# Graph-network layer: the overflow of two grouped quads in one accumulation, and remainders, ranks, splits and lists at other places of the hand-written order

## The chip, the cores and the metric

The kernel runs on one core of a Trainium2 chip. A core has five engines that run side by side, each with a queue of its own in program order: TensorE (PE, with PEld for its weight loads), VectorE (DVE), ScalarE (ACT), GpSimd (POOL) and SyncE (SP, which here only issues DMAs). The metric is device microseconds of one launch, as the median of several runs. The profile is of one further execution of the same program.

## What is computed

The reference is one message-passing layer on a graph of 6,250 nodes and 200,000 edges, sorted by `dst`:

```python
h = relu(layernorm(x)) @ W_in
W_ij = (softplus_shifted(f_ij @ W_f1 + b_f1) @ W_f2 + b_f2) * f_ij_cutoff
out = segment_sum(h[dst] * W_ij, src, 6250)      # a random scatter-add of 200,000 rows of 128
result = x + softplus_shifted(out @ W_o1 + b_o1) @ W_o2 + b_o2
```

`edge_index` is `[src, dst]`, so the messages are gathered by the sorted index and summed by the random one. The scatter-add of 200,000 rows of 128 numbers is what most of the kernel is about.

## The kernel before

**Items.** The edges are cut into 391 quads of 512 edges (four chunks of 128). The main loop (from line 1220 on) runs over items `i`. In item `i` the quads near `i` are each at another stage: `s1_*` makes the softplus of the edge features of quad `i` (PE `z` on line 326, ACT on lines 331 and 336), `s2_*` the message of quad `i-1` (PE `xg` and `W` on lines 507 to 518, ACT `xc` on line 523, and on line 533 the product of `W` and `xc` on DVE, `s2_m`), `s3_*` the rest of quad `i-2` to `i-4`. What else has to run is hung on an item and on a point of it with `at(item, point, function)`: L (loads), D0, D1, A0, A1, DM, PE2, A2, D2, S, run in this order of the code. The order is kept as written on every engine, so a function that is hung on an early point stands ahead of everything that comes later in the item on its engine.

**Three ways to sum a message.** 31 quads are plain: equal sources inside a chunk are summed with a matmul and each chunk is added into DRAM with one indirect DMA of POOL (line 595). 192 quads are listed: each of their four chunks is added with one such DMA straight from the product, and duplicate sources are moved into a list of 128 rows that is summed on its own (`l_*`; `l_eq` on line 382 compares, two instructions for four quads). 168 quads are grouped, with no DMA of their own: 128-row chunks are sorted on TensorE into 16 groups of 32 slots by a one-hot matrix `pm` (`perm_oh`, `permute`, line 700), and every eight of them make a round of four units (`unit_oh`, `unit_pe` on line 794, `unit_evac` on line 805) that add 32 slots of each group into the SBUF table `accT`. All indirect adds go through one POOL queue: 987 DMAs in the run.

**The grid of nine.** Grouped quads start at item 8 with gaps of 2, 2, 2 and 3. With phase = (item - 8) mod 9 they are at the phases 0, 2, 4 and 6. Units sit in items of phase 2 and 6 (`UOFF`); `clear` pushes a step to the next item that has no unit.

**The functions around the change.** A grouped quad `q` gets its product in item `q+1` into `pt` (two buffers, `part_new`). The product is kept as three bf16 pieces that lie in the high halves of f32 numbers: `part_rem` (line 689) makes two remainders, in item `q+2` at D2, and `part_ext` adds three index columns; a row of `pt` then has 387 columns. `permute` runs in the items `q+3` and `q+4`. Slots beyond the 16 x 32 go to 64 overflow slots of the quad: `over_pe` (lines 708 to 718) sums the three pieces of each of four chunks with twelve matmuls of 64 columns of weights into one half of a PSUM tile, `over_out` copies 64 x 131 numbers to one half of `mo`, and after every second grouped quad `over_idx`, `over_dg`, `over_row`, `over_eq`, `over_sum` (line 754, f32) and `over_scatter` sum equal rows of `mo` and add them to DRAM with one DMA. PSUM tiles of the tag `B` have four buffers, which `permute`, the units, the overflow and most side work share.

**The side work.** `rank_group`, `rank_count`, `rank_own`, `rank_over`, `rank_slot` make the slots of eight grouped quads at once, ahead of the first of them. `fb_load`, `fb_1` to `fb_4` split 4,096 edges' features in three bf16 pieces every eight items; `fb_2` also takes their largest absolute value (line 287). `unit_oh` makes the eight one-hot matrices of a unit, four two items ahead and four one item ahead. A list's `l_eq` and `l_count` run in the first items that have its data.

Of the kernel before, what the change touches and what calls it, by code (L numbers as in the profile page):

```python
# [54 lines left out]
def tile_gnn(ctx: ExitStack, tc: tile.TileContext, x, fB, cT, srcT, srcr, dstr, win_, wf1, wf2, bias, bo1c, wo1,  # L55
# [113 lines left out]

    def zero_list(k, j):  # L170
        v = accs[k][ACC_R:].rearrange("(p t) f -> p (t f)", p=P)
        w = LR // ZL
        nc.sync.dma_start(v[:, j * w:(j + 1) * w], zero[:, :w])

    def rows(t, o, T):
        n = min(T, 2)
# [104 lines left out]
    def fb_1(b):  # L281
        f3 = wk.tile([P, 3, FE], BF16, tag="f3", name="f3", bufs=2)
        nc.scalar.copy(f3[:, 0], fst[b]["f"])
        fst[b]["f3"] = f3

    def fb_2(b):
        nc.vector.tensor_reduce(fmax[:, b:b + 1], fst[b]["f"], axis=AX.X, op=ALU.max, apply_absolute_value=True)
# [418 lines left out]
        nc.scalar.copy(mp[q]["ms", s][:, :PW], mp[q].pop(("q", s))[:, :PW])  # L706

    def over_pe(q):
        h = mpi[q] % 2 * OVC
        t = ps.tile([P, 512], F32, tag="B", name="po", bufs=4)  # L710
        o = t[h:h + OVC]
        for c in range(4):
            w = mp[q]["pm"][:, c, GRP * CAP:]
            pt = high(mp[q]["pt"][:, c:c + 1])[:, 0]
            nc.tensor.matmul(o[:, :P + 3], w, pt[:, 2 * P:PW], start=(c == 0), stop=False)  # L715
            nc.tensor.matmul(o[:, :P], w, pt[:, P:2 * P], start=False, stop=False)  # L716
            nc.tensor.matmul(o[:, :P], w, pt[:, :P], start=False, stop=(c == 3))  # L717
        mp[q]["po"] = t

    def over_out(q):  # L720
        h = mpi[q] % 2 * OVC
        mo = mos[mpi[q] // 2 % 2]
        nc.scalar.copy(mo[h:h + OVC, :P + 3], mp[q].pop("po")[h:h + OVC, :P + 3])

    def over_none(q):
        nc.vector.memset(mos[mpi[q] // 2 % 2][OVC:, :P + 3], 0.0)

    def over_idx(q):
        mo = mos[mpi[q] // 2 % 2]
        so = sp_.tile([P, 1], F32, tag="ovs", name="ovs", bufs=3)  # L730
        nc.vector.scalar_tensor_tensor(so, mo[:, P + 2:P + 3], float(GN), mo[:, P + 1:P + 2], op0=ALU.mult, op1=ALU.add)
        mp[q]["so"] = so

    def over_dg(q):
# [10 lines left out]
        mp[q]["row"] = t  # L745

    def over_eq(q):
        eq = wk.tile([P, P], F32, tag="oeq", name="oeq", bufs=1)
        nc.vector.tensor_scalar(eq, mp[q].pop("row")[:, :P], mp[q]["so"], None, op0=ALU.is_equal)
        mp[q]["eq"] = eq  # L750

    def over_sum(q):
        t = ps.tile([P, 512], F32, tag="B", name="osum", bufs=4)
        nc.tensor.matmul(t[:, :P + 4], mp[q]["eq"], mos[mpi[q] // 2 % 2][:, :P + 4], start=True, stop=True)
        mp[q]["sum"] = t

    def over_copy(q):
# [91 lines left out]
    with tc.manual_schedule():  # L849
# [70 lines left out]
        fb_1(0)  # L920
        prep_norm(0)
        prep_tp(0)
        fb_2(0)
        prep_relu(0)
        prep_mm(0)
# [22 lines left out]
            nc.vector.tensor_copy(m_[:, :, 128:129], wgt.unsqueeze(1).to_broadcast([P, 4, 1]))  # L948
            ms.append(m_)
        for mo_ in mos:  # L950
            nc.vector.tensor_copy(mo_[:, P + 3:P + 4], wgt)
        idl = cp.tile([P, max(NW, 1)], F32, name="idl")
        iotl = cp.tile([P, P + LCAP], F16, name="iotl")
        nc.vector.tensor_scalar(iotl, iotw[:, GN // 2:GN // 2 + P + LCAP], float(LCAP - 1), None, op0=ALU.subtract)
# [183 lines left out]
        for w in range((LE - LB) // SW):  # L1138
            for g in range(4):
                n = LB + SW * (w - 1) + 4 * g  # L1140
                i = splain[n] + 2 if w else 6 + 2 * g
                for k in range(2):
                    kk = (LB + SW * w + 4 * g) // 2 + k
                    at(max(0, i + k - 2), "L", sb_load, kk)
                    at(i + k, "DM", l_eq, kk)
                i = clear(i + 2, units)
                at(i, "PE2", l_count, (LB + SW * w) // 4 + g)
                at(i + 1, "D0", l_dup, w, g)
            i += 1
# [12 lines left out]
            at(i, "PE2", over_row, ("L", w))  # L1162
            at(i + 1, "D0", l_same, w)
            k = clear(i + 1, units)
            at(k - 1, "L", l_load, w)
            at(k, "PE2", l_sum, w)
            at(k + 1, "A0", l_copy, w)
            at(k + 1, "DM", l_ji, w)
            at(k + 1, "A2", over_int, ("L", w))
            at(k + 2, "S", over_scatter, ("L", w))  # L1170
# [3 lines left out]
                    at((0, 3, 6, 9)[k] + j + 1, "L", zero_list, k, j)  # L1174
        for q in mpq:
            at(q + 1, "D2", perm_oh, q)
            at(q + 2, "D2", part_rem, q, 1)
            at(q + 2, "D2", part_rem, q, 2)
            at(q + 2, "A2", part_ext, q)
            if q + 4 in units:  # L1180
                for s in range(4):
                    at(q + 3, "PE2", permute, q, s)
                for s in range(4):
                    at(q + 3, "PE2", perm_out, q, s)
                at(q + 3, "PE2", over_pe, q)
                at(q + 3, "PE2", over_out, q)
# [6 lines left out]
            if q == mpq[-1] and mpi[q] % 2 == 0:  # L1193
                at(q + 4, "D2", over_none, q)
# [25 lines left out]
        for i in range(max(NQ + 7, last + 16, r0_end + 2, lend + 24)):  # L1220
# [396 lines left out]
```

## Time and profile before

| | |
|---|---|
| median of 3 runs | 2064.37 us (2062.51 to 2069.87) |
| the profiled execution's own time | 2051.26 us |
| its span | 2049.5 us |
| PE, DVE, ACT, POOL busy | 1855.4, 1658.4, 1491.2, 1636.9 us |
| mean granted TensorE clock | 0.966 |
| indirect adds of POOL (line 595) | 987, of 1.59 to 1.64 us each |
| permutation matmuls (line 700) | 2688, 533.6 us |
| overflow matmuls (lines 715 to 717) | 3 x 672, 131.3 + 127.2 + 127.4 us |

Busy times of PE are modelled ends of pipelined matmuls and overlap; the distance from one start to the next tells what a matmul takes of the engine. "Issue" after an idle time means that the engine waited for nothing that the profile shows. A row of the timeline has the start in us, the length in us, the engine, the line, the operation, its tiles and shapes, how many were merged, and in brackets the idle time ahead of it and what ended it.

### The profile page before, as it was taken

How to read it: one execution, taken by the hardware profiler on the slowest of the kernel's cores; microseconds unless marked ns; L12 is line 12 of the kernel's file. 1: busy time of each engine (PE TensorE's matmuls, PEld its weight loads, DVE VectorE, ACT ScalarE, POOL GpSimd, SP SyncE). 2: the span in 40 equal slices, each digit the busy share in tenths (PEclk: the TensorE clock that was granted, in tenths of full speed). 3: DMA queues.
4: the chain of work that ended last, by engine and by line, in shares of the span. 5: the costliest groups of instructions: out<-in, count | busy, mean ns of one | idle time of the engine just before them, and what ended most of it. 6: DMA issues, size and time to landing. Idle time of an engine off the chain costs nothing. (4 is left out here: it accounts for less than half of the span.)

```text
span 2049.5 us, 57496 instructions
## 1 busy us (share of the span) xinstructions
PE 1855.4 (91%) x20381; PEld 1284.7 (63%) x20381; DVE 1658.4 (81%) x4449; ACT 1491.2 (73%) x4083; POOL 1636.9 (80%) x1040
## 2 busy tenths in 40 slices
PE   3579999999999999999999999999999999999966
PEld 2456666666666666666666666666666666677734
DVE  4578898798888888988888978879898887787745
ACT  3468776877777788777778777777877778788714
POOL 3578888888888888887878778888888888888884
PEclk9689999999999999999999999999999999999987
DMA  6887666667666676766667666676676666666747
GB/s 239 228 210 154 124 123 121 129 110 140 126 126 119 118 139 119 131 127 120 120 121 132 120 117 123 110 125 127 121 131 108 129 126 109 112 123 125 141 44 252
DMA packets 359686, 272.58 MB, mean 133 GB/s; under 512 B 97727, under 2 KB 319850, under 8 KB 359394
## 3 DMA queue, kind: packets, MB, share of 16 engines
q0 software_dynamic: 143728, 71.30, 34.9%
q1 hardware_dynamic: 215378, 197.50, 32.9%
q8 instruction: 161, 2.64, 0.5%
q14 instruction: 131, 1.07, 0.2%
q10 hardware_dynamic: 288, 0.07, 0.0%
HBM read 154.45 MB, written 114.24 MB: 131 GB/s over the span
## 5 line engine op out<-in xcount | busy, mean ns | idle before, releaser
L595 POOL DMA_INDIRECT acc<-s,lji x768 | 1242.7, 1618 | 254.5 <-issue 185.8
L700 PE MATMUL pq<-pt,pm 128*128 128x387 bf16 x2688 | 533.6, 342 | 33.6 <-DVE pt L689 10.5
L523 ACT ACTIVATE xc<-xg,cb 128x128 f32<-128x128 f32 x1564 | 447.7, 372 | 111.5 <-PE xg L510 101.8
L518 PE MATMUL W<-w,a 128*128 128x128 f32 x3128 | 465.3, 293 | 0.0
L518 PEld LDWEIGHTS W<-w,a 128*128 128x128 f32 x3128 | 389.6, 196 | 42.3 <-issue 3.1
L706 ACT CAST mst<-pq 128x387 bf16<-128x387 f32 x672 | 303.7, 482 | 135.0 <-PE pq L700 132.3
L700 PEld LDWEIGHTS <-pm 128*128 128x128 bf16 x2688 | 261.0, 99 | 221.5 <-issue 26.6
L794 PE MATMUL un<-so,mst 32*128 32x392 bf16 x8064 | 371.0, 326 | 12.9 <-DVE pr L640 6.4
L794 PEld LDWEIGHTS <-mst 32*128 32x128 bf16 x8064 | 223.9, 93 | 153.4 <-issue 51.0
L336 ACT ACTIVATE a<-a,con 128x512 f32<-128x512 f32 x391 | 282.3, 722 | 12.8
L331 ACT ACTIVATE a<-z 128x512 f32<-128x512 f32 x391 | 237.8, 608 | 32.9 <-PE z L326 18.0
L595 POOL DMA_INDIRECT acc<-s,ji x123 | 196.0, 1594 | 78.7 <-issue 26.5
L689 DVE TENSOR_TENSOR pt<-pt 128x512 f32<-128x512 f32 x336 | 231.7, 689 | 5.8
L675 DVE TENSOR_SCALAR pm<-iot,pos 128x576 bf16<-128x576 f16 x672 | 221.0, 390 | 0.0
L533 DVE TENSOR_TENSOR s<-W,xc 128x512 f32<-128x512 f32 x192 | 131.9, 687 | 89.1 <-ACT xc L523 84.9
L805 DVE TENSOR_TENSOR accT<-un,accT 128x392 f32<-128x392 f32 x320 | 158.5, 558 | 55.1 <-PE un L794 55.0
L779 DVE TENSOR_SCALAR so<-iot,mst 128x392 bf16<-128x392 f16 x672 | 192.6, 346 | 5.4 <-PE un L794 5.3
L595 POOL DMA_INDIRECT acc<-os,oji x96 | 156.9, 1635 | 30.7 <-issue 15.6
L510 PE MATMUL xg<-wn,oh 63*128 63x128 bf16 x1564 | 157.5, 222 | 14.8 <-ACT xc L523 8.2
L326 PE MATMUL z<-ft,ws 123*128 123x512 bf16 x391 | 151.9, 389 | 15.7 <-POOL b2rep L940 9.3
L507 PE MATMUL W<-b2rep,onesb 64*128 64x512 bf16 x391 | 154.1, 394 | 0.0
L533 DVE TENSOR_TENSOR pt<-W,xc 128x512 f32<-128x512 f32 x168 | 115.3, 686 | 44.1 <-ACT xc L523 36.0
(210 smaller groups left out, 2431.3 us busy)
## 6 DMA issues: line engine op xcount, KB each, us to landing
rb<-reld SPq DMA_DIRECT2D x391, 64.0 KB
fsd<-f SPq DMA_DIRECT2D x49, 480.0 KB
ft<-fsd SPq DMA_DIRECT2D x195, 120.0 KB
sb<-src SPq DMA_DIRECT2D x169, 128.0 KB
fb<-in_fB_dram SPq DMA_DIRECT2D x49, 320.0 KB
ft<-fsd SPq DMA_DIRECT2D x195, 80.0 KB
wn<-tab SPq DMA_DIRECT2D x782, 15.8 KB
acc<-s,lji POOLq DMA_INDIRECT x768
```

What stands on the lines that cost most here:

```text
L331: nc.scalar.activation(a, st[q]["z"], AF.Exp)
L336: nc.scalar.activation(a, a, AF.Ln, bias=half, scale=0.5)
L518: nc.tensor.matmul(W[:, c, :], st[q]["a"][:, c * P:(c + 1) * P], w2, start=False, stop=(c == 3))
L523: nc.scalar.mul(xc[:, c, :], st[q]["xg"][:, c, :], late["c", q // CQ][:, 4 * (q % CQ) + c:4 * (q % CQ) + c + 1])
L533: nc.vector.tensor_tensor(m[:, :, :P], st[q]["W"], st[q]["xc"], op=ALU.mult)
L595: nc.gpsimd.indirect_dma_start(out=accs[k][:rows, :], out_offset=bass.IndirectOffsetOnAxis(ap=ji, axis=0), in_=s, in_offset=None, compute_ ...
L675: nc.vector.tensor_scalar(pm[:, c], iot[:, :SLOTS], rk[r]["pos"][:, 4 * j + c:4 * j + c + 1], None, op0=ALU.is_equal)
L689: nc.vector.tensor_tensor(pt[:, :, k * P:(k + 1) * P], a, high(a), op=ALU.subtract)
L700: nc.tensor.matmul(t[:, :PW], mp[q]["pm"][:, c, s * P:(s + 1) * P], high(mp[q]["pt"][:, c:c + 1, :PW])[:, 0], start=(c == 0), stop=(c == 3))
L706: nc.scalar.copy(mp[q]["ms", s][:, :PW], mp[q].pop(("q", s))[:, :PW])
L779: nc.vector.tensor_scalar(so, iotw[:, :GN], w[:, 3 * P // 2:3 * P // 2 + 1], None, op0=ALU.is_equal)
L794: nc.tensor.matmul(ts[g][:, :GN], mp[q]["ms", s][v, k * P:(k + 1) * P], mp[q]["oh"][v], start=(q == qs[0] and k == 0), stop=(q == qs[-1] a ...
```

## The change

- `over_pe` runs once for two grouped quads (84 times): for each of the four chunks one matmul of 387 columns per quad, the first quad into the lower and the second into the upper 64 partitions of the PSUM tile, so that the matmuls go to the two halves of the array's columns in turn. The three pieces are no longer added in PSUM.
- `over_out` copies all 387 columns of both quads at once to `mo`, which becomes bf16; `over_sum` adds the three pieces with three bf16 matmuls; the one-hot `oeq` becomes bf16. `over_none` goes.
- `over_pe` and `over_out` move to a new point PE1, behind `s2_m` and ahead of `s3_pe`, of the item after the next grouped quad (phases 5 and 1). `part_rem` moves from D2 to a new point DR, right behind the product.
- `rank_group`, `rank_count` and `rank_own` run one item sooner.
- The maximum of the splits becomes `fb_max` and runs three items ahead of `fb_2`; the loads come six items ahead and no longer three; the splits start one item ahead of a unit, the lists' compares in a unit's item.
- The first half of `unit_oh` moves to the item of the second half for units of phase 6.
- The launch asks for `dynamic_dma_scratch_size=8192`, where before it named no size.

```diff
-        mo_ = cp.tile([P, 132], F32, name=f"mo{i}")
+        mo_ = cp.tile([P, PW + 1], BF16, name=f"mo{i}")
...
     def over_pe(q):
-        h = mpi[q] % 2 * OVC
+        qs = mpq[mpi[q] // 2 * 2:mpi[q] + 1]
         t = ps.tile([P, 512], F32, tag="B", name="po", bufs=4)
-        o = t[h:h + OVC]
         for c in range(4):
-            w = mp[q]["pm"][:, c, GRP * CAP:]
-            pt = high(mp[q]["pt"][:, c:c + 1])[:, 0]
-            nc.tensor.matmul(o[:, :P + 3], w, pt[:, 2 * P:PW], start=(c == 0), stop=False)
-            nc.tensor.matmul(o[:, :P], w, pt[:, P:2 * P], start=False, stop=False)
-            nc.tensor.matmul(o[:, :P], w, pt[:, :P], start=False, stop=(c == 3))
-        mp[q]["po"] = t
+            for h, p in enumerate(qs):
+                nc.tensor.matmul(t[h * OVC:(h + 1) * OVC, :PW], mp[p]["pm"][:, c, GRP * CAP:],
+                                 high(mp[p]["pt"][:, c:c + 1, :PW])[:, 0], start=(c == 0), stop=(c == 3))
+        mp[q]["po"] = t, len(qs) * OVC
...
     def over_out(q):
-        nc.scalar.copy(mo[h:h + OVC, :P + 3], mp[q].pop("po")[h:h + OVC, :P + 3])
+        nc.scalar.copy(mo[:n, :PW], t[:n, :PW])
...
     def over_sum(q):
-        nc.tensor.matmul(t[:, :P + 4], mp[q]["eq"], mos[mpi[q] // 2 % 2][:, :P + 4], start=True, stop=True)
+        nc.tensor.matmul(t[:, :P + 4], mp[q]["eq"], mo[:, 2 * P:], start=True, stop=False)
+        nc.tensor.matmul(t[:, :P], mp[q]["eq"], mo[:, P:2 * P], start=False, stop=False)
+        nc.tensor.matmul(t[:, :P], mp[q]["eq"], mo[:, :P], start=False, stop=True)
...
         for b in range(1, NB):
-            t0 = 2 if b == 1 else 8 * b - 8
+            t0 = 2
             if b > 1:
-                at(max(0, t0 - 3), "L", fb_load, b)
+                t0 = 8 * b - 8
+                while (t0 - MP0 + 1) % sum(MPGAPS) not in UOFF:
+                    t0 -= 1
+                at(max(0, t0 - 6), "L", fb_load, b)
+            at(max(t0 - 3, 1), "D2", fb_max, b)
...
-            at(i - 5, "D2", rank_group, r)
-            k = clear(i - 4, units)
-            at(k, "PE2", rank_count, r)
-            at(k + 1, "D0", rank_own, r)
-            k = clear(k + 1, units)
+            i = max(i, 6)
+            at(i - 6, "D2", rank_group, r)
+            at(i - 5, "PE2", rank_count, r)
+            at(i - 4, "D0", rank_own, r)
+            k = mpq[RKQ * r] if i == 6 else i - 2
             at(k, "PE2", rank_over, r)
             at(k + 1, "D0", rank_slot, r)
...
                 i = splain[n] + 2 if w else 6 + 2 * g
+                while w and (i - MP0) % sum(MPGAPS) not in UOFF:
+                    i -= 1
...
-            at(q + 2, "D2", part_rem, q, 1)
-            at(q + 2, "D2", part_rem, q, 2)
+            at(q + 2, "DR", part_rem, q, 1)
+            at(q + 2, "DR", part_rem, q, 2)
...
-                at(q + 4, "PE2", over_pe, q)
-                at(q + 5, "A0", over_out, q)
...
             if mpi[q] % 2 or q == mpq[-1]:
+                k = mpq[mpi[q] + 1] + 1 if mpi[q] + 1 < len(mpq) else q + 3
+                at(k, "PE1", over_pe, q)
+                at(k, "PE1", over_out, q)
...
-                at(k - 2, "D2", unit_oh, r, s, 0)
+                at(k - (1 if (k - MP0) % sum(MPGAPS) == UOFF[1] and k < last else 2), "D2", unit_oh, r, s, 0)
...
                 s3_idx(i - 3)
+            run(i, "DR")
+            run(i, "PE1")
...
-    nc = bacc.Bacc("TRN2", target_bir_lowering=False, num_devices=1)
+    nc = bacc.Bacc("TRN2", target_bir_lowering=False, num_devices=1, dynamic_dma_scratch_size=8192)
```

More of the change, by code (lines that the diff above doesn't have):

```diff
@@ L171, in zero_list @@
         v = accs[k][ACC_R:].rearrange("(p t) f -> p (t f)", p=P)
-        w = LR // ZL
-        nc.sync.dma_start(v[:, j * w:(j + 1) * w], zero[:, :w])
+        a, b = j * LR // ZL, (j + 1) * LR // ZL
+        nc.sync.dma_start(v[:, a:b], zero[:, :b - a])
     def rows(t, o, T):
@@ L284, in fb_1, with fb_max @@
         fst[b]["f3"] = f3
+    def fb_max(b):
+        nc.vector.tensor_reduce(fmax[:, b:b + 1], fst[b]["f"], axis=AX.X, op=ALU.max, apply_absolute_value=True)
     def fb_2(b):
-        nc.vector.tensor_reduce(fmax[:, b:b + 1], fst[b]["f"], axis=AX.X, op=ALU.max, apply_absolute_value=True)
         fr = wk.tile([P, FE], F32, tag="fr", name="fr", bufs=1)
@@ L708, in over_pe @@
     def over_pe(q):
[L709 removed]
+        qs = mpq[mpi[q] // 2 * 2:mpi[q] + 1]
         t = ps.tile([P, 512], F32, tag="B", name="po", bufs=4)
[L711 removed]
         for c in range(4):
[L713 to L718 removed]
+            for h, p in enumerate(qs):
+                nc.tensor.matmul(t[h * OVC:(h + 1) * OVC, :PW], mp[p]["pm"][:, c, GRP * CAP:],
+                                 high(mp[p]["pt"][:, c:c + 1, :PW])[:, 0], start=(c == 0), stop=(c == 3))
+        mp[q]["po"] = t, len(qs) * OVC
     def over_out(q):
[L721 removed]
+        t, n = mp[q].pop("po")
         mo = mos[mpi[q] // 2 % 2]
[L723 to L726 removed]
+        nc.scalar.copy(mo[:n, :PW], t[:n, :PW])
+        if n < P:
+            nc.vector.memset(mo[n:, :PW], 0.0)
     def over_idx(q):
@@ L730, in over_idx @@
         so = sp_.tile([P, 1], F32, tag="ovs", name="ovs", bufs=3)
-        nc.vector.scalar_tensor_tensor(so, mo[:, P + 2:P + 3], float(GN), mo[:, P + 1:P + 2], op0=ALU.mult, op1=ALU.add)
+        nc.vector.scalar_tensor_tensor(so, mo[:, PW - 1:PW], float(GN), mo[:, PW - 2:PW - 1], op0=ALU.mult, op1=ALU.add)
         mp[q]["so"] = so
@@ L747, in over_eq @@
     def over_eq(q):
-        eq = wk.tile([P, P], F32, tag="oeq", name="oeq", bufs=1)
+        eq = wk.tile([P, P], BF16, tag="oeq", name="oeq", bufs=1)
         nc.vector.tensor_scalar(eq, mp[q].pop("row")[:, :P], mp[q]["so"], None, op0=ALU.is_equal)
@@ L922, in tile_gnn @@
         prep_tp(0)
+        fb_max(0)
         fb_2(0)
@@ L950, in tile_gnn @@
         for mo_ in mos:
-            nc.vector.tensor_copy(mo_[:, P + 3:P + 4], wgt)
+            nc.vector.tensor_copy(mo_[:, PW:PW + 1], wgt)
         idl = cp.tile([P, max(NW, 1)], F32, name="idl")
@@ L1184, in tile_gnn @@
                     at(q + 3, "PE2", perm_out, q, s)
-                at(q + 3, "PE2", over_pe, q)
-                at(q + 3, "PE2", over_out, q)
             else:
```

3 lines of the change are left out of this document (1 added, 2 removed).

## The prediction, made before the result was known

> **What bounds the kernel now.** The page comes first, for the sizes, then the stretches of the run by engine, then what POOL waited for in each.
>
> ```profile
> span 2049.5 us, 57496 instructions
> PE 1855.4 (91%) x20381; PEld 1284.7 (63%) x20381; DVE 1658.4 (81%) x4449; ACT 1491.2 (73%) x4083; POOL 1636.9 (80%) x1040
> ```
>
> PE looks like the bound and POOL, at 80%, does not. But the page does not count a gap that POOL has between every two indirect adds. The stretches (length; then busy us and instructions of PE, PEld, DVE, ACT, POOL; granted clock, DMA share, GB/s) and POOL's waits (us, times, longest) in the first of them:
>
> ```profile
> 150.00:1206.00 1056.00, 991.19 (x11115) 680.65 (x11114) 903.92 (x2512) 806.89 (x2230) 869.59 (x536) 0.98 0.68 126
> 1206.00:1880.00 674.00, 653.33 (x7446) 449.94 (x7445) 568.50 (x1483) 528.56 (x1448) 566.89 (x351) 1.00 0.67 121
> 1880.00:1950.00 70.00, 68.58 (x713) 51.33 (x714) 52.25 (x128) 57.20 (x165) 57.29 (x36) 1.00 0.69 131
> ...
> POOL acc L595 <- issue: 124.5, 408, 0.3
> POOL acc L595 <- DVE s L533: 17.6, 13, 4.1
> POOL acc L595 <- DMA acc<-s,lji: 16.1, 42, 1.5
> POOL acc L595 <- DVE bn L199: 4.6, 4, 1.8
> ```
>
> An issue gap is 124.5 / 408 = 0.305 us and stands ahead of every add, whatever the row calls its end. With it POOL's stretches are: 869.59 + 536 x 0.305 = 1033.1 of 1056 us, 566.89 + 351 x 0.305 = 673.9 of 674, and 57.29 + 36 x 0.305 = 68.3 of 70. So from 1206 to 1880 POOL had no free microsecond, and in 1800 us it had 22.9 + 0.1 + 1.7 = 24.7 free. PE is 991.19 + 653.33 + 68.58 = 1713.1 of the same 1800 us, 95%. Two engines are at their limit side by side: PE in the first 1056 us, where POOL still waits for products, POOL behind that. The end says the same (durations in ns, then the first and the last start of the overflow's last line, and POOL's last add):
>
> ```profile
> L717 PE MATMUL po<-pt,pm x672: 218/220/312, 119.1 to 1941.2; 128*64 128x128 bf16 x168
> ...
> 1994.96 1.54 POOL L595 DMA_INDIRECT acc<-os,oji  x1 [0.30 <-issue]
> ```
>
> PE is done with the last overflow at 1941.2 us; POOL still works on a queue of adds until 1994.96 + 1.54 = 1996.5, and only then the last stage can load the sums. The change takes away no add: 987 stay. **So what it can give is the time that POOL waits, at most 24.7 us, however much PE saves.**
>
> **The change, part by part.** *The overflow on PE.*
>
> ```profile
> 1008.75 1.56 PE L700 MATMUL pq<-pt,pm 128*128 128x387 bf16 x8
> 1010.24 0.25 PE L715 MATMUL po<-pt,pm 128*64 128x131 bf16 x1
> ...
> 1011.08 0.39 PE L507 MATMUL W<-b2rep,onesb 64*128 64x512 bf16 x1
> 1019.35 4.45 PE L794 MATMUL un<-so,mst 32*128 32x392 bf16 x96
> 1023.73 0.39 PE L507 MATMUL W<-b2rep,onesb 64*128 64x512 bf16 x1
> ```
>
> Starts count. Twelve overflow matmuls take 1011.08 - 1010.24 = 0.84 us, at most 0.07 each; I count 0.06 each and 0.12 for the change of shape. Two quads take 1.68. A matmul of 387 columns takes (1010.24 - 1008.75) / 8 = 0.186. The new form has eight of these for two quads. No row shows two halves of the columns in turn. Bounds: one after the other, 8 x 0.186 + 0.12 = 1.61, a gain of 0.07; both halves at once, 4 x 0.186 + 0.12 = 0.86, a gain of 0.82. The nearest row is the unit: matmuls on four different quarters of the rows go at (1023.73 - 1019.35) / 96 = 0.046 us each, four in the time of one. So I take the second: 84 x 0.82 = 69 us of PE.
>
> ```profile
> L715 PEld LDWEIGHTS <-pm 128*64 128x64 bf16 x672 | 72.5, 108 | 57.6 <-issue 56.6 <-DVE rt L664 0.7 <-DVE dropT L668 0.3
> ```
>
> A weight load of 64 columns takes 108 ns, yet these matmuls start 60 ns apart: loads lie under running matmuls. The Trainium skill, in "TensorE: Matmul & The Clock Gate", Part 3, "The mechanism", says that a weight load overlaps matmuls in flight only when its row group differs; here all twelve use the same rows, so for one half of the columns the trace speaks against it, and for halves in turn no run shows it. By that rule the 69 us would be a loss; that is the fourth case below.
>
> *The sum of equal rows, and the copies.*
>
> ```profile
> 1036.58 0.39 PE L754 MATMUL osum<-mo,oeq 128*128 128x132 f32 x2
> 1036.81 1.56 PE L700 MATMUL pq<-pt,pm 128*128 128x387 bf16 x8
> L723 ACT COPY mo<-po 64x131 f32<-64x131 f32 x168 | 44.1, 263 | 34.9 <-PE po L717 30.2 <-issue 0.8
> L706 ACT CAST mst<-pq 128x387 bf16<-128x387 f32 x672 | 303.7, 482 | 135.0 <-PE pq L700 132.3 <-issue 0.4
> ```
>
> The f32 sum took 0.23; three bf16 matmuls at the overflow's 0.06 take 0.18: 84 x 0.05 = 4 us of PE. ACT made 168 copies of 263 ns and now makes 84 like L706's, of 482: 44.1 - 40.5 = 4 us less. The new copy stands behind ACT's `xc`, when the overflow is long done, so most of the 30.2 us wait goes too. ACT is at 77% in these stretches, so neither reaches the end. The memset in `over_out` never runs, with 168 grouped quads.
>
> *The wait that is added.* At phases 5 and 1 the product of a third grouped quad asks for a `pt` buffer while the first quad's is still to be read by `over_pe`, which stands behind it in the item. So DVE must wait for PE at `s2_m`, and behind it stand its remainders, `perm_oh`, `unit_oh` and the next product, for which POOL waits.
>
> ```profile
> 1035.65 1.23 DVE L382 TENSOR_TENSOR eql<-sb,srcT_sb 128x1024 bf16<-128x1024 int16 x1 [0.25 <-DMA sb<-src]
> 1036.79 0.69 DVE L533 TENSOR_TENSOR pt<-W,xc 128x512 f32<-128x512 f32 x1
> ...
> 1012.62 0.54 PE L391 MATMUL lcnt<-wgtb,eql 128*128 128x1 bf16 x16
> ...
> 1014.78 0.68 DVE L533 TENSOR_TENSOR pt<-W,xc 128x512 f32<-128x512 f32 x1
> ```
>
> The first two rows are a phase 1. PE would start `over_pe` where `osum` starts now, at 1036.58, done at 1036.58 + 0.86 = 1037.44, 0.65 us behind the product's present start. The other two are a phase 5: `over_pe` would start in place of the work at 1012.62 and end at 1013.48, over a microsecond ahead of the product, so nothing. Per grid of nine at most 0.65 us, 42 times: 27 us of DVE, which is idle for 1800 - (903.92 + 568.50 + 52.25) = 275 us. I take zero on the path, as a product one microsecond late is hidden as long as POOL has another one queued, and keep 27 as the other end.
>
> *The moves.*
>
> ```profile
> L689 DVE TENSOR_TENSOR pt<-pt 128x512 f32<-128x512 f32 x336 | 231.7, 689 | 5.8
> L779 DVE TENSOR_SCALAR so<-iot,mst 128x392 bf16<-128x392 f16 x672 | 192.6, 346 | 5.4 <-PE un L794 5.3
> ```
>
> No instruction is added or dropped here, so only stalls change. `part_rem` (two of 689 ns, L689) gets ahead of splits, ranks and one-hots, so that `permute` and `over_pe` find it done; ranks one item sooner free a unit's item from `rank_own`. The first half of `unit_oh` (four of 346 ns, L779) comes later, but ahead of the second, and a unit spends 4.38 / 8 = 0.55 us on each of its eight, longer than DVE needs to make one. `l_eq` and the splits go where PE is busy for 4.4 us with a unit. The loads come sooner on the same queue, with DMA at 0.68. All this lies in PE's or DVE's slack: zero. The DMA scratch can't be seen in any row; POOL waits for landings only 16.1 - 42 x 0.305 = 3.3 us in the first stretch, so I take zero.
>
> *The start.* One move is not free. `fb_max` of the third split is now in item 1, and its load in item 0 behind the zeroing.
>
> ```profile
> 38.21 1.23 SPq L278 DMA_DIRECT2D fb<-in_fB_dram  x1
> ...
> 47.19 0.45 SPq L357 DMA_DIRECT2D sb<-src  x1
> 44.20 0.72 ACT L283 CAST f<-fb 128x640 bf16<-128x640 f32 x1 [6.79 <-DMA fb<-in_fB_dram]
> 53.83 0.22 DVE L569 SCALAR_TENSOR_TENSOR jf<-s,con,jd 128x4 f32<-128x4 f32 x1
> 56.82 0.81 DVE L297 TENSOR_TENSOR f<-fr,f 128x640 bf16<-128x640 f32 x1
> 65.35 0.41 SPq L298 DMA_DIRECT2D fsd<-f  x1
> 83.49 1.23 DVE L382 TENSOR_TENSOR eql<-sb,srcT_sb 128x1024 bf16<-128x1024 int16 x1 [9.74 <-DMA sb<-src]
> ```
>
> SP would issue that load at about 47.2; the one before took 44.2 - 38.2 = 6 us to land; so DVE would stand in item 1 until 53.2, and `jf`, which releases the first add and is at 53.83 now, would come some 6 us later (an estimate: the landing, as the work between stays). But DVE waits 9.74 us at 83.49 for a list's load. The one thing ahead of that load on SP which the delay reaches is the write of the second split, ready at 57.6 and issued at 65.35, so it has 7.7 us to spare. That swallows the delay. I take zero and keep 6.
>
> *The sum.* PE needs 69 + 4 = 73 us less where POOL has 24.7 to give. Of POOL's waits in the first stretch, those for DVE and its product can go: 17.6 + 4.6 - 17 x 0.305 = 17.0 us. The landing waits (3.3) and odd ones stay. So 2051.3 - 17 = 2034.3 for the profiled execution. Its own time is 13.1 us under the median of the runs, 2064.4, so the forecast is 2064.4 - 17 = **2047.4**.
>
> **The rivals.** *Halves one after the other.* PE saves 84 x 0.07 + 4 = 10 us instead of 73, and only the part in the first stretch tells: 10 x 1056 / 1800 = 6 us, 2058. For it: every overflow matmul in the trace uses one half of the columns at a time, and both halves read all 128 rows, which the unit's quarters do not. Against it: nothing in the rows. The Trainium skill's "TensorE: Matmul & The Clock Gate", Part 3, "Measured speedup vs the span model", gives 2.38 for three column tiles, which is for the forecast; no run here shows it.
>
> *DVE waits for `over_pe`* (ends slower). Place: `s2_m` at phase 1. Price: 27 us of DVE. It decides as soon as POOL has no product queued at that item, so that each wait is passed on to an add: 2064.4 + 27 - 17 = 2074. Against it: POOL went 674 us without one wait for a product, so it has some in stock. For it: in the first stretch it had 13 waits for one.
>
> *Weight loads exposed* (slower). If a load for one half can't lie under the other half's matmul, two quads take 8 x (0.108 + 0.186) + 0.12 = 2.47 us in place of 1.68, 66 us more PE in all. PE has 1800 - 1713 = 87 us left, of which most is waits for others, so with some 10 us of them used it gives 2064.4 + 66 - 10 = 2120.
>
> **How the numbers follow.** Forecast 0.58, halves in turn 0.24, the `pt` wait 0.11, exposed loads 0.07. The forecast's own range is 2036 to 2056: all 24.7 us and 4 of scatter on one side, the start's 6 us and some waits left on the other. The range for 8 in 10 adds the second case and the third's 2074: 2036 to 2076; outside it lie the fourth case and some of the third. About 0.5% (10 us) is what a measurement of this kernel can tell from no change. Faster by more (below 2054.0): the forecast but for 0.06 of it, 0.52. Within: that 0.06, the second case and a little of the third, 0.33. Slower: 0.15.
>
> **What would show it.** Right: `po` has 672 matmuls, and eight of them start within 0.9 us; PE busy falls by some 70 us in starts while POOL, with an issue gap of 0.305 counted, is above 99% from 150 us to the last add; POOL's row for "DVE s" nearly goes, and DVE gets waits for "DMA acc" at `s` instead, as the four `s` buffers fill up. Wrong: eight `po` in 1.5 us; a row of DVE `pt` waiting for PE `po` with tens of us; a first add later than 60 us and no wait left at the list's load. The forecast fails above all if adds become longer or shorter than their mean of 1.62 us: 987 of them turn each 0.01 us into 10.

## The result, and the profile after

| | before | after |
|---|---|---|
| median beside each other, 22 runs each | 2065.54 us (2056.34 to 2072.47) | 2061.21 us (2053.47 to 2071.24) |
| ratio of after to before | | 0.9984, 95% interval 0.9971 to 0.9998 |
| the profiled execution's own time | 2051.26 us | 2063.64 us |
| indirect adds: first start, last start | 54.66, 1994.96 us | 57.78, 2007.27 us |

The change takes 3.3 us off by the ratio, where 17 were forecast. That is within 0.5%, about no change. A second pair in a later batch gave 1.0015 (1.0002 to 1.0028), so nothing was gained there. The changed kernel took 2061.21 and 2060.86 us in the two; it was the kernel before that differed, 2065.54 and 2056.57 us.

First the page after: the span, the engines and POOL's three groups of adds (busy us, mean ns of one, idle time ahead of them).

```profile
span 2061.9 us, 54889 instructions
PE 1820.4 (88%) x19121; PEld 1188.1 (58%) x19121; DVE 1650.9 (80%) x4449; ACT 1470.8 (71%) x3999; POOL 1652.4 (80%) x1040
...
L597 POOL DMA_INDIRECT acc<-s,lji x768 | 1254.4, 1633 | 250.4 <-issue 185.5
L597 POOL DMA_INDIRECT acc<-s,ji x123 | 198.4, 1613 | 80.1 <-issue 26.7
L597 POOL DMA_INDIRECT acc<-os,oji x96 | 158.1, 1647 | 30.4 <-issue 18.3
```

The same three groups of the kernel before:

```profile
L595 POOL DMA_INDIRECT acc<-s,lji x768 | 1242.7, 1618 | 254.5 <-issue 185.8
L595 POOL DMA_INDIRECT acc<-s,ji x123 | 196.0, 1594 | 78.7 <-issue 26.5
L595 POOL DMA_INDIRECT acc<-os,oji x96 | 156.9, 1635 | 30.7 <-issue 15.6
```

PE has 1260 matmuls less. But POOL, with the same 987 adds, is *busier*: 1610.9 against 1595.6 us. All three groups have become longer by 12 to 19 ns an add. These are means: the median add takes 1.54 us in both kernels, and 241 adds of before and 270 of after take more than 0.06 us longer than that, some over 2.5 us.

The stretches of after (length; busy us and instructions of PE, PEld, DVE, ACT, POOL; clock, DMA share, GB/s), then POOL's waits from 150 to 1206 us:

```profile
150.00:1206.00 1056.00, 971.79 (x10359) 624.75 (x10361) 898.25 (x2507) 795.75 (x2184) 874.14 (x536) 0.97 0.68 125
1206.00:1880.00 674.00, 629.69 (x6868) 406.89 (x6857) 555.86 (x1462) 514.31 (x1395) 567.85 (x348) 0.97 0.66 119
1880.00:1960.00 80.00, 78.61 (x835) 55.94 (x836) 60.46 (x152) 64.35 (x184) 65.54 (x42) 1.00 0.70 128
```

```profile
POOL acc L597 <- issue: 125.4, 407, 1.6
POOL acc L597 <- DVE s L535: 12.4, 9, 3.3
POOL acc L597 <- DMA acc<-s,lji: 11.7, 32, 0.9
```

With 0.305 us for each add POOL's three stretches are 1037.6 of 1056, 674.0 of 674 and 78.4 of 80 us: 1790.0 of 1810, 98.9%. The wait for the product, which was nearly to go, is 12.4 us where it was 17.6. POOL is still the bound, and it now has less free time but more to do. The granted clock of TensorE fell too, from 1.00 to 0.97 in the second stretch, but POOL has no free time there in either kernel, so a slower PE took nothing from it there.

PE's timeline of after, at one phase 5:

```profile
1021.78 0.89 PE L715 MATMUL po<-pt,pm 128*64 128x387 bf16 x8
1022.60 0.23 PE L753 MATMUL osum<-mo,oeq 128*128 128x132 bf16 x1
1022.66 0.22 PE L754 MATMUL osum<-mo,oeq 128*128 128x128 bf16 x1
1022.72 0.22 PE L755 MATMUL osum<-mo,oeq 128*128 128x128 bf16 x1
1022.78 2.96 PE L702 MATMUL pq<-pt,pm 128*128 128x387 bf16 x16
```

Eight overflow matmuls take 1022.60 - 1021.78 = 0.82 us, so the halves run at once (0.86 was forecast), and the three of `osum` take 0.06 each. So it is in 77 of the 84 pairs, in under 0.9 us: the second half's matmul starts 4 ns behind the first half's, the next two some 0.17 us later (medians). PE's part came out as worked out.

### The profile page after: what moved, and what is told of

Read it like the earlier page. It is cut to its first block, busy times and chain, and to the rows that moved or that the text cites. A ratio compares the mean times of both kernels' runs of the same rounds, so it can differ in the third digit from the quotient of the medians.

```text
span 2061.9 us, 54889 instructions
## 1 busy us (share of the span) xinstructions
PE 1820.4 (88%) x19121; PEld 1188.1 (58%) x19121; DVE 1650.9 (80%) x4449; ACT 1470.8 (71%) x3999; POOL 1652.4 (80%) x1040
## 3 DMA queue, kind: packets, MB, share of 16 engines
q8 instruction: 151, 2.47, 0.5%
## 4 chain that ended last, share of the span: by engine, by line
PE 46%; DVE 20%; ACT 10%; DMA 7%; issue 6%; POOL 5%; SPq 4%; DVEq 0%; ACTq 0%; POOLq 0%
PE pq L702 15%; PE W L520 10%; PE un L795 8%; POOL acc L597 5%; ACT xc L525 3%; PE po L715 2%; DVE accT L806 2%; DVE pt L691 2%; PE z L328 2%; ACT mst L708 2%; DVE eql L384 2%; PE xg L512 2%; DMA acc<-s,lji 2%; DVE pm L677 2%; ACT a L333 2%
## 5 line engine op out<-in xcount | busy, mean ns | idle before, releaser
L702 PE MATMUL pq<-pt,pm 128*128 128x387 bf16 x2688 | 545.6, 346 | 43.2 <-ACT pt L697 10.6
L338 ACT ACTIVATE a<-a,con 128x512 f32<-128x512 f32 x391 | 282.3, 722 | 12.7
L535 DVE TENSOR_TENSOR pt<-W,xc 128x512 f32<-128x512 f32 x168 | 115.5, 687 | 132.4 <-PE po L715 62.9
L780 DVE TENSOR_SCALAR so<-iot,mst 128x392 bf16<-128x392 f16 x672 | 181.2, 333 | 9.7 <-PE un L795 9.2
L328 PE MATMUL z<-ft,ws 123*128 123x512 bf16 x391 | 151.7, 388 | 15.5 <-POOL b2rep L942 9.3
```

The lines of the kernel that those rows point to most:

```text
L338: nc.scalar.activation(a, a, AF.Ln, bias=half, scale=0.5)
L535: nc.vector.tensor_tensor(m[:, :, :P], st[q]["W"], st[q]["xc"], op=ALU.mult)
L702: nc.tensor.matmul(t[:, :PW], mp[q]["pm"][:, c, s * P:(s + 1) * P], high(mp[q]["pt"][:, c:c + 1, :PW])[:, 0], start=(c == 0), stop=(c == 3))
```

## One account for all runs

POOL runs nothing but these adds from the first to the last, so the time can be split: **first add** (its start in POOL's timeline), **adds** (the 987 durations, the sum of POOL's three groups), **gaps** (986 x 0.305 = 300.7 us; the median gap is 0.305 us in every kernel) and **waits** (what is left up to the start of the last add). From its start to the end of the run it is 2049.5 - 1994.96 = 54.5 us before, 2061.9 - 2007.27 = 54.6 after, and 52.6 to 54.6 in all. So only three numbers can differ by more than 2 us. Here they are for every profile of a kernel with 987 adds (us):

| kernel | first add | adds | waits | last add |
|---|---|---|---|---|
| before (the profile shown) | 54.7 | 1595.6 | 45.5 | 1995.0 |
| b_same (before again) | 55.0 | 1596.3 | 61.9 | 2012.3 |
| after | 57.8 | 1610.8 | 39.5 | 2007.3 |
| a_same (after again) | 58.2 | 1618.1 | 41.9 | 2017.4 |
| after_again | 57.6 | 1604.2 | 40.1 | 2001.1 |
| scratch | 54.7 | 1598.3 | 59.1 | 2011.3 |
| overflow_only | 54.6 | 1602.1 | 50.7 | 2006.6 |
| moves_only | 57.7 | 1615.6 | 63.2 | 2035.7 |
| remainders_only | 54.3 | 1594.6 | 75.0 | 2023.0 |
| splits_only | 57.7 | 1601.1 | 53.7 | 2011.7 |
| lists_only | 54.7 | 1606.5 | 72.8 | 2033.1 |
| third_pt | 58.3 | 1608.7 | 39.2 | 2005.4 |
| overflow_rem | 54.7 | 1594.8 | 51.1 | 1999.8 |
| overflow_rem_again | 55.6 | 1599.1 | 50.8 | 2004.7 |
| no_lists | 58.0 | 1599.5 | 40.0 | 1996.7 |
| one_input | 58.6 | 1577.6 | 67.7 | 2003.0 |
| ov_rem_one_input | 54.3 | 1576.9 | 74.8 | 2005.2 |
| ov_rem_rank_oh | 54.0 | 1600.3 | 44.9 | 1998.3 |

Means of before (two profiles) and after (three): waits 53.7 to 40.5, **13 us gained**. Adds 1596.0 to 1611.0, **15 us lost**. First add **3 us** later. Together they are 5 us more in these profiles, about nothing. The two profiles of before differ by 16 us in waits alone, and three of after by 14 in adds, so one profile tells no difference of 5 us; what the runs below decide, they decide by medians and intervals. Against the one profile that the forecast was made from, after has only 6 us less of waits, 15 more of adds and 3 more at the start.

## The experiments

**Theory:** POOL's queue of adds is the bound; the overflow does what was forecast, and the moves take it back, by longer adds and by delayed products. **Rivals:** the new wait of the product for `over_pe`; the scratch; simply too little to gain on POOL's side.

*The same two kernels once more* (b_same, a_same, and after_again with the last run).

> The kernel before, unchanged, for a second profile. Theory (the run is as long as its 987 indirect adds): mean add 1.61 to 1.63 us, and the time moves with the mean add by 987 times the difference; no wait of POOL between 1206 and 1880 us. Rival (PE sets the end): the mean add may be anything, and POOL shows waits for products all along.

> The changed kernel, unchanged, for a second profile. Theory A (the change makes adds longer, because DVE work now falls together with them): mean add near 1.631 us again, some 0.015 above the kernel before on the same chip. Theory B (the mean add differs from run to run): it may lie at 1.615 as well. Both: three waits of DVE for the overflow product come to some 60 us in all, POOL's free time about 18 us in the first stretch.

2067.61 and 2072.82 us. The sum of adds is 1596.3 against 1595.6 us for before, and 1618.1 against 1610.8 for after (1604.2 in after_again). So the longer adds belong to the changed kernel and are not one profile's chance. What differs between the two profiles of before is POOL's waits, 45.5 and 61.9 us, 12 us of it between 500 and 850 us; the forecast was read from the shorter one.

*Is POOL the bound?* (b_few, a_few.) The fourth chunk of the listed quads is not added: 795 adds instead of 987.

```diff
-        scat[q + (2 if LB <= plain[q] < LE else 4)] += min(4, NCH - 4 * q)
+        scat[q + (2 if LB <= plain[q] < LE else 4)] += min(3 if LB <= plain[q] < LE else 4, NCH - 4 * q)
...
-            for c in range(nchunks(q)):
+            for c in range(3):
```

> The kernel before, without the add of the fourth chunk of each of the 192 listed quads (that part of the sum is left out), 795 adds in place of 987. POOL then needs 370 us less, so what is left is PE with its own waits. Theory (PE was the bound in the first stretch and POOL overall): 2064 less 15 to 60 us. Rival (POOL alone is the bound): far faster, by 150 us or more.

> The changed kernel, without the same 192 adds. Theory (PE's saving of some 73 us is real and POOL hides it): 45 to 75 us below the kernel before without these adds. Rival (the saving is eaten by new waits between PE, DVE and ACT, above all DVE's wait for the overflow product): within 20 us of it.

Before 2045.72 us, 0.9904 (0.987 to 0.9937); after 2016.49 us, 0.9775 (0.9736 to 0.9815). POOL's waits in b_few, then in a_few, and one of DVE's waits in a_few:

```profile
POOL acc L595 <- DVE s L533: 254.8, 89, 7.6
```

```profile
POOL acc L597 <- DVE s L535: 313.6, 112, 6.4
```

```profile
DVE pt L535 <- PE po L715: 68.2, 36, 5.0
```

Before gains 20 us, after 45: with POOL relieved the change is worth 2045.7 - 2016.5 = 29 us, not 3. So some 26 us of what it saves is hidden by POOL. That before gains only 20 us, of some 370 that POOL has less to do, says also that the chain which makes the products stands only 20 us behind POOL. And of the 73 us that PE was to save only 29 show even here. POOL now waits for products for hundreds of microseconds, and the product itself waits for `over_pe`: some 24 of the 68.2 us lie behind the end of both `W` and `xc`, and the rest it would wait anyway. The work of PE, ACT and DVE is chained; where the rest of the 73 us went was not taken apart.

*The parts alone.* Scratch: before with `dynamic_dma_scratch_size=8192`, nothing else.

> The kernel before with dynamic_dma_scratch_size=8192 alone. Two profiles of the kernel before have a mean add of 1.615 us, two of the changed kernel 1.631 and 1.638. Theory S (the smaller scratch makes adds longer): 1.63 to 1.64 here, and 15 to 22 us slower than before. Theory M (where DVE's instructions lie against the adds) and theory O (the overflow's new form): 1.615, no change of time.

0.9997 (0.9978 to 1.0015): nothing. The rival falls.

Overflow_only takes `over_pe`, `over_out`, `over_sum`, PE1 and the scratch; moves_only takes all other edits, with the old overflow.

> The kernel before with the paired overflow, its copy, its bf16 sum, its place PE1 and the smaller scratch, without any of the moves of remainders, ranks, splits, lists and one-hots. Theory O: mean add 1.63 or more. Theory M: 1.615, and so 10 to 20 us faster than before, as POOL's waits for products go. Theory S: as the run with the scratch alone, less up to 17.

> The kernel before with all moves (remainders, ranks, splits and their maxima, lists, one-hots), without the new overflow and with the old scratch. Theory M: mean add 1.63 or more and some 15 us slower than before, as PE saves nothing. Theories S and O: 1.615 and within 6 us of before. All: the first add some 3 us later, from the maximum that waits for its load.

Overflow alone 2058.97 us, 0.9955 (0.9932 to 0.9978); the moves alone 2092.93 us, 1.0129 (1.0097 to 1.016). So edits which were put down at zero cost 26 us where they stand alone. The table says where: adds 1615.6 (20 over before's), first add 3 us later, waits 63.2 (10 over the mean of before).

*Which move?* One each, on the kernel before: remainders at DR; splits with `fb_max`; lists at units.

```diff
-            at(q + 2, "D2", part_rem, q, 1)
-            at(q + 2, "D2", part_rem, q, 2)
+            at(q + 2, "DR", part_rem, q, 1)
+            at(q + 2, "DR", part_rem, q, 2)
...
+                while w and (i - MP0) % sum(MPGAPS) not in UOFF:
+                    i -= 1
```

> The kernel before with the remainders right behind the product, and nothing else. All moves together made the mean add 1.635 us, from 1.615, and the run 26 us slower. Theory M1 (the remainders do it: 336 long f32 instructions with two SBUF inputs now run back to back with the product): mean add 1.625 to 1.635, 8 to 20 us slower. Rival M2 (splits or lists do it): 1.615 and within 5 us of before.

> The kernel before with the splits' maxima, loads and places of the change, and nothing else. Theory M2: the splits, which now stand with the unit, lengthen adds: mean add above 1.62 and 5 us or more slower; the first add 3 us later, from the maximum that waits for its load. Rival M1: mean add 1.615; within 4 us of before, of which 3 us at the start.

> The kernel before with the lists' compares at units, and nothing else. Theory M2: mean add above 1.62 and 5 us or more slower. Rival M1: mean add 1.615 and within 4 us of before.

Remainders 1.0089 (1.0069 to 1.0108), splits 1.0005 (0.9987 to 1.0022), lists 1.0099 (1.0075 to 1.0123). POOL's waits from 150 to 1206 us in remainders_only, then in lists_only:

```profile
POOL acc L595 <- DVE s L533: 38.4, 20, 4.6
```

```profile
POOL acc L595 <- issue: 117.8, 386, 0.3
POOL acc L595 <- DVE s L533: 23.4, 12, 3.7
POOL acc L595 <- DVE bn L199: 18.2, 8, 4.0
```

With the remainders right behind a product POOL stands longer for products: the wait for `s` is 38.4 us where it was 17.6 (20.2 in b_same), and the adds are not longer (1594.6). So M1 had the place right and the mechanism wrong. The lists lengthen POOL's waits too (72.8 us in all) and the adds by 11 us. The splits delay the first add by 3 us; the interval of their time is too wide to tell 3 us from none.

*The added wait* (third_pt): after with a third `pt` buffer.

```diff
-        mp.setdefault(q, {})["pt"] = wk.tile([P, 4, PW], F32, tag="pt", name="pt")
+        mp.setdefault(q, {})["pt"] = wk.tile([P, 4, PW], F32, tag="pt", name="pt", bufs=3)
```

> The changed kernel with a third buffer for the product pt, so that DVE's product needn't wait for the overflow. DVE's wait of 63 us for the overflow goes. If that wait costs time: 10 to 30 us faster than the changed kernel. If the length of the adds sets the time: within 5 us of it, and the mean add at 1.63.

DVE's idle time ahead of `pt` in after (all of it, and the part that `over_pe` ended), then the same row with three buffers:

```profile
L535 DVE TENSOR_TENSOR pt<-W,xc 128x512 f32<-128x512 f32 x168 | 115.5, 687 | 132.4 <-PE po L715 62.9
```

```profile
L535 DVE TENSOR_TENSOR pt<-W,xc 128x512 f32<-128x512 f32 x168 | 115.1, 685 | 101.3 <-ACT xc L525 60.8
```

The 62.9 us (34 waits) is not the price of the overflow: it is DVE's whole idle time ahead of these products, and most of it would have been spent on `W` and `xc`. The third buffer takes 132.4 - 101.3 = 31 us away. What lies behind the end of both `W` and `xc` in the trace is 20 us of the 62.9, 0.6 a wait (21 and 31 us in a_same and after_again, by the same reckoning). So the price is near the 27 us of the prediction, but it is paid at both phases, in 19 waits at 5 and 15 at 1; in all 34 the overflow's first matmul runs without a gap behind the item's `W` and `z`. The time with three buffers is 2061.59 us, 0.9977 (0.9962 to 0.9992), the same as after. So the rival has its place and its size, and still costs nothing that shows.

*Overflow and remainders together* (overflow_rem), and the same beside after on one chip (overflow_rem_again, after_again).

> The paired overflow with the remainders right behind the product and the smaller scratch, without the moves of ranks, splits, lists and one-hots. With the remainders late, PE waited 41 us for them ahead of the overflow; that wait goes. If it cost time and the remainders don't lengthen adds: 5 to 15 us below the overflow alone (2059), 15 to 22 below before, which is the most that POOL has to give. If the remainders lengthen adds (M1): level with the overflow alone or slower, mean add above 1.625.

> The changed kernel as it is, timed beside the next one on one chip. Theory (the moves cost: lists at units lengthen adds and delay the product): ratio to before 0.998, 3 to 4 us faster, mean add 1.63 to 1.64 us. Rival (the chips differ, and the change is worth what its best parts are worth): 0.993 to 0.995 as overflow_rem had elsewhere.

> Overflow in pairs and remainders early alone, beside the changed kernel on one chip. Theory: 6 to 12 us shorter than the changed kernel (0.993 to 0.996 of before), mean add 1.614 us. Rival (the earlier 0.9935 was that chip's): within 3 us of the changed kernel, 0.997 to 0.999 of before.

Overflow_rem 2053.68 us, 0.9935 (0.9921 to 0.995). Side by side: after 2060.86 us, 1.0015 (1.0002 to 1.0028); overflow_rem 2054.35 us, 0.9972 (0.9957 to 0.9986). For after 0.998 of before and adds of 1.63 us or more were expected, and 1.0015 and 1.625 came; the 6 to 12 us between the two kernels came as expected, the 0.993 to 0.996 of before did not. The intervals lie apart: without its other moves the change is 6.5 us faster than with them, and 0.3% faster than the kernel before. The account gives the same: from the two profiles of overflow_rem to the three of after, adds are 14 us longer, the first add is 3 us later and waits are 10 us shorter. So in the whole change the other moves do not delay products, as the theory had it; they help there, and the longer adds cost more than that. What the early remainders do here is in PE's waits, overflow_only first, then overflow_rem:

```profile
PE po L713 <- DVE pt L689: 41.3, 26, 3.9
```

```profile
PE po L713 <- DVE pt L689: 6.2, 8, 1.4
```

The overflow at PE1 waits 41.3 us for remainders that come at D2. So the same move costs 18 us without the new overflow and costs nothing with it; that it pays there is not shown, as 0.9955 and 0.9935 come from two batches and their intervals overlap.

*After without the lists* (no_lists), *and overflow_rem with ranks and one-hots* (ov_rem_rank_oh).

> The changed kernel with the lists' compares where they were before. The lists' move alone cost 21 us and made the mean add 1.626 us. If it is what spoils the change: mean add 1.61 to 1.62 and 2045 to 2055 us, as the overflow with the remainders (2054) or better. If the moves of ranks, splits and one-hots spoil it: near the changed kernel, 2057 to 2062.

> The overflow with the remainders and the smaller scratch, and the ranks and one-hots moved as well, without splits and lists. If ranks and one-hots help as they are meant to: below 2054, PE's 17 us wait of units for the ranks gone, mean add 1.615. If they cost: above 2054, with more waits of POOL for products.

2052.24 us, 0.9985 (0.9968 to 1.0002), and 2051.2 us, 0.9975 (0.9958 to 0.9992), in a batch where before took 2056.89. Taking the lists back makes after some 9 us shorter (2060.86 to 2052.24, batches with before at 2056.6 and 2056.9; the two intervals just touch), with 1599.5 us of adds instead of 1604 to 1618 and the same waits. The ranks and one-hots cost nothing that shows, and PE's wait of 17.3 us for the ranks ahead of units is gone.

*Why adds become longer* (one_input, ov_rem_one_input). DVE's timeline of after, and POOL's for the same times:

```profile
659.97 1.22 DVE L384 TENSOR_TENSOR eql<-sb,srcT_sb 128x1024 bf16<-128x1024 int16 x1
...
788.11 1.21 DVE L384 TENSOR_TENSOR eql<-sb,srcT_sb 128x1024 bf16<-128x1024 int16 x1
```

```profile
660.99 1.61 POOL L597 DMA_INDIRECT acc<-os,oji  x1 [0.30 <-issue]
...
788.14 2.59 POOL L597 DMA_INDIRECT acc<-os,oji  x1 [0.31 <-issue]
```

The add at 788.14 starts 0.03 us into a compare and takes 2.59 us, that at 660.99 starts 1.02 into one and takes 1.61. Both end 1.41 us after the compare's end: 790.73 - 789.32 and 662.60 - 661.19. Of the adds that begin 0.03 us or more into such a compare, 59 of 61 in after and 49 of 51 in b_same end 1.41 to 1.48 us behind it; the other four begin in its last 0.06 us and take their 1.54. So an add that begins in a compare stands until the compare is over. The Trainium skill, in "SBUF — State Buffer", "Who interferes with whom", has the rule: a DVE instruction with two inputs in SBUF contends with a GpSimd instruction that reads SBUF, and the second one blocks wholly. The compare has two inputs in SBUF, the add reads its row numbers there, and the 1.41 us agrees with a block, not with sharing. (The same section infers that a `tensor_tensor` does not hold up a DMA that GpSimd issues; these adds are such DMAs and are held, so that does not stand here.) The trace has a second test: 105 adds of after begin under the product (`W` in PSUM, `xc` in SBUF) and 92 under `accT` (`un` in PSUM), also instructions with two tensors, and all of them together are 0.5 us longer than at 1.542 each. If it is the second input in SBUF, a compare with one input in SBUF and a scalar for each partition should not do it:

```diff
-        nc.vector.tensor_tensor(eq, sbs.pop(k).rearrange("p (c i) -> p c i", c=8),
-                                srcT_sb[:, n * 4:n * 4 + 8].unsqueeze(2).to_broadcast([P, 8, P]), op=ALU.is_equal)
+        sf = sp_.tile([P, 8], F32, tag="lsf", name="lsf", bufs=2)
+        nc.vector.tensor_copy(sf, srcT_sb[:, n * 4:n * 4 + 8])
+        v = sbs.pop(k)
+        for c in range(8):
+            nc.vector.tensor_scalar(eq[:, c], v[:, c * P:(c + 1) * P], sf[:, c:c + 1], None, op0=ALU.is_equal)
```

> The changed kernel with each list compare as eight DVE instructions of 128 columns with one SBUF tensor and a scalar per partition, in place of one of 1024 columns with two SBUF tensors; the same result, some 50 us more of DVE. Adds that start under the compare with two tensors last 2.1 to 2.2 us in place of 1.54. If DVE's second SBUF input holds POOL up: that excess of some 30 us goes, mean add 1.60 to 1.61 in place of 1.631 to 1.638. If any DVE work does it: the mean add stays above 1.625.

> The overflow with the remainders and the smaller scratch, with the lists where they were, and the same eight compares with one SBUF tensor. By the second input: mean add 1.585 to 1.595 in place of 1.614, 20 us less for 987 adds; the time falls by that less what 50 us more of DVE cost, 2040 to 2055. Otherwise mean add 1.61 and slower than 2054 by DVE's 50 us in part.

The adds fall to 1577.6 and 1576.9 us (1.598 each, where 1.585 to 1.595 was expected of the second), 26.6 us or more below after's and 17.9 or more below overflow_rem's, and of the 69 adds of one_input that begin under a compare 3 are more than 0.06 us longer than 1.542. So the block by this compare is shown. The time does not fall: 2060.86 us, 1.0022 (1.0008 to 1.0036), and 2055.14 us, 0.9989 (0.9973 to 1.0006). One_input's compares and its POOL's wait (150 to 1206 us) tell why:

```profile
L388 DVE TENSOR_SCALAR eql<-sb,lsf 128x128 bf16<-128x128 int16 x768 | 138.7, 288 | 19.4 <-DMA sb<-src 15.7 <-PE lcnt L396 0.5
```

```profile
POOL acc L600 <- DVE s L538: 43.0, 26, 4.0
```

DVE is 1690.7 us busy on its page where after's has 1650.9, products come later, and POOL waits for them what it saved: waits 67.7 against 40.5. With shorter adds the chain that makes products is the bound.

*Which instructions hold the adds in the whole change?* Here is the time by which adds exceed 1.542 us, summed by the DVE instruction that runs when the add starts:

| us over 1.542 an add | before, b_same | after, a_same, after_again | no_lists |
|---|---|---|---|
| one-hots (`pm`, `so`, `oh`) | 7.1, 7.6 | 14.9, 15.9, 12.7 | 10.4 |
| lists' and plain compares | 28.9, 30.2 | 33.0, 35.3, 29.4 | 29.8 |
| remainders | 24.3, 22.4 | 24.3, 28.3, 25.3 | 21.4 |
| splits | 8.8, 8.2 | 10.8, 10.0, 9.2 | 10.7 |
| all else, and DVE idle | 4.6, 6.0 | 6.0, 6.7, 5.7 | 5.3 |

Of the 270 long adds of after 253 end 1.40 to 1.45 us behind the end of a DVE instruction, of the 241 of before 236; by chance it would be one in eight (4449 instructions, a window of 0.055 us, in 2062 us). The largest part of the 15 us is under the one-hots, 7 us. In after `so` stands 39 times in a row of eight, where before has four at most, and an add can stand through several of them (DVE, then POOL):

```profile
1797.47 1.94 DVE L780 TENSOR_SCALAR so<-iot,mst 128x392 bf16<-128x392 f16 x8
```

```profile
1797.38 2.41 POOL L597 DMA_INDIRECT acc<-s,lji  x1 [0.30 <-issue]
```

These are instructions with one tensor and a scalar, as the eight compares are, but from 16-bit floats. Why they hold an add and the eight compares do not is not tested here. The rows of eight alone are not it: ov_rem_rank_oh has them too, and 8.9 us under its one-hots.

## Why the prediction was wrong, point by point

- **The bound: right.** POOL's adds with their gap hold the time. 192 adds less gave 20 and 45 us, and most of PE's saving did not pass through. But the chain that makes the products is only some 20 us behind (b_few), and with shorter adds it holds the time (one_input).
- **The overflow on PE: right.** 0.82 us for two quads (0.86 forecast), halves at once; *halves one after the other* (1.61) and *exposed loads* (2.47) are out. By the rule of the Trainium skill's "TensorE: Matmul & The Clock Gate", Part 3, "The mechanism", loads would have been exposed here, as all eight matmuls use the same rows; the 0.82 us speaks against it for halves of the columns in turn.
- **What POOL's waits can give: a term that was too large.** All 17.0 us of waits for DVE and its product from 150 to 1206 us were to go. Counted in the same way, beyond the gap, POOL's waits for DVE there are 17.3 us in before and 11.4, 15.5 and 13.0 in the three profiles of after: 2 to 6 went, and the row for `s`, which was nearly to go, still has 12.4 us. That the account's means give 13 us, near the forecast, is luck: b_same has 28.8 us of these waits.
- **The start: right in the place, half in size.** The first add is 3 us later (6 was the estimate). That it is swallowed, as said, is not shown: splits_only gives 1.0005, with an interval that holds 3 us.
- **The added wait: right in size and effect, wrong in its place.** At most 27 us, at phase 1 only, was worked out; the third buffer takes 31 us off, and the waits are at both phases. The row of tens of microseconds that was to speak against the forecast came, and most of it is time that DVE waits for `W` and `xc` anyway. Third_pt shows that it is not on the path.
- **The moves: this step failed.** "All this lies in PE's or DVE's slack: zero" was read off each engine's own free time. Moves_only measures 26 us, remainders_only 18, lists_only 20. Alone, the moves lengthen POOL's waits for products (remainders, lists) and its adds (lists). In the whole change the waits do not grow; the moves beyond the remainders cost 6.5 us there, by adds that are 14 us longer, and the lists are most of it (9 us, no_lists). DVE's idle time was the wrong measure: where an instruction of DVE lies against POOL's adds has a price too.
- **The length of an add: the term that was missing.** The sum had it constant, and named it as what could fail. It rose from 1.617 to 1.632, 1.639 and 1.625 us (sums by 987), 8 to 22 us of 987 adds, on average 15 of the 17 us that were forecast.

What stays open: how each move sets which adds fall under which instruction. Without the lists' move the adds are 11.5 us shorter, spread over one-hots, remainders and compares (4, 5 and 3 us against after's means, one profile), so it does more than shift its own compares; how was not traced. Open too is why the kernel before took some 2066 us in most batches and 2057 in two, while after and overflow_rem kept theirs; against the second, after is 0.15% slower and not faster.

## What to carry to other kernels

Look for the engine whose queue never stands still once its issue gaps are counted, and then hold its own instruction's length to be a result of what runs beside it, not a constant: 987 instructions turn 15 ns into the whole gain. A move inside another engine's idle time is not free if it lands ahead of what the bound waits for, or beside an instruction of the bound that it holds up. Split a change into its parts and run them alone and together, as a part may cost by itself and cost nothing beside another (the remainders). And an idle time that one engine ended is not what that engine costs: ask what the wait would have ended on otherwise (62.9 us here, and without the cause DVE's idle time fell by 31).

## What the hardware showed that was not expected

- An indirect DMA add of POOL that begins 0.03 us or more into a DVE compare with two inputs in SBUF stands until that ends, and itself ends 1.41 to 1.48 us later (108 of 112 such adds in two profiles; the others begin at its very end); undisturbed it takes 1.54 us. Under DVE instructions with one of two inputs in PSUM it is not held (197 adds of after, 0.5 us in all). With one tensor and a scalar the mean add fell from 1.632 (1.625 in the shortest profile) to 1.598 us. One-hots from 16-bit floats hold adds too: the one shown took 2.41 us.
- Matmuls of 64 columns of weights in turn to the lower and the upper 64 output partitions: eight of 128x387 bf16 in 0.82 us, 0.10 each, where one full matmul of 387 columns takes 0.186.
- DMA scratch of 8192, where no size was named before: 0.9997 (0.9978 to 1.0015).
